# Where the second input's normalizations run, and which PSUM bank takes the first group's adapter products

## The chip, the cores and the metric

The kernel runs on one core of a Trainium2 chip. The metric is the device time of one execution in microseconds (us), as a median over executions. The engines are named as in the profile: PE (TensorE, matrix products), DVE (VectorE), ACT (ScalarE), POOL (GpSimd) and SP (SyncE, which only issues DMAs here). PSUM is the memory that PE writes its products to; the kernel uses it in banks of 128 x 512 float32.

## The reference

Two inputs x[b] of 1024 rows and 1024 columns, all in float32, go through four layers: causal attention with 32 heads of 32 and a small adapter, a feed-forward layer with a router, a second attention, and the feed-forward layer again. The change lies in the first one:

```python
x = x + attn_a(layernorm(x), w_attn, w_proj, adapter_wte, gating)

qkv = x @ w_attn.T                      # q, k, v: 32 heads of 32
q, k = rope(q), rope(k)
y = softmax(causal(q @ k.T / sqrt(32))) @ v
aq, ak, av = adapter_wte @ w_attn.T     # 10 adapter rows; ak and av are used
y = y + gating * softmax(q @ ak.T / sqrt(1024)) @ av
return y @ w_proj.T
```

The layer norm takes the mean and the variance of each row and has no weights.

## The kernel before, in words

**Attention A** works on 2 inputs (b) x 8 groups of four heads (g) x 2 halves of 512 queries (n), one `Unit` each, in that order. `attend` walks over the units in rounds. A round issues score products (tiles `sc` and `st`, two buffers in all), then the products with v, then `late`, and then it spends a fixed budget on other PE work. This other work stands in a queue of generators, the `Filler`: `project(b, g)` makes q, k and v of a group, as many groups ahead as a gate allows. Each `yield` of a number is a piece of PE work with that cost; a yielded tuple costs nothing and only marks that something is done.

**Order.** PE's and POOL's instructions keep the order in which the program writes them in this stage. The instructions of DVE, ACT and SP are put in order by the compiler's scheduler, which works by its own estimate of when operands are ready, so they can run long before their place in the program. An instruction given to `tc.keep_in_program_order` is issued behind the instruction that stands before it on its engine.

**Layer norm.** `layernorm` (L241) takes a tile of 128 rows: two `bn_stats` (L244), an aggregate (L248), a small step (L251), two steps on ACT (L253, L255), three small steps (L257 to L259) and the normalized tile (L261). With `behind=True` the first `bn_stats` alone is held in program order.

**The second input.** `normalize_ahead` (L719) loads each of its eight tiles, normalizes it and stores it to DRAM (`xnd`, L723). From group 3 to group 6 the main loop (L1002 to L1009) adds two tiles ahead of the group's projection. The tiles have the tag `t4k`, with three buffers for loads and results together. Later `second` (L727) loads the normalized tiles back and transposes them on PE, two steps a tile, into `xnT[1, n]`. `project_blocks(0, 7)` takes eight of these steps and `project_first(1)` the other eight, through `next(turnover)`.

**The banks.** Short work takes a bank from `bank` (one buffer, tag `ps`): transposes of the second input, the adapter's scores (`asc`) and their transpose, the adapter's parts, and the rows of shifts. Products of the projections take one of a pair, `ca` and `cb`: `next_bank` swaps the pair and gives the one that was used less recently, `block_bank` gives one without a swap. The adapter's keys (`akp`) and values (`avp`) are short products: before, those of group 0 take `next_bank`, those of later groups `block_bank`.

**The start.** All eight tiles of the first input are normalized; four are transposed (`half(0, 0)`, alternating banks of the pair); then `project_first(0)` makes k, the adapter's keys, q, and in `values_first` the adapter's parts and v with the adapter's values; then come the other four tiles and their products. `rotate` (L806) reads k or q from its bank on DVE (L811, L812) and ends on POOL (L815, L816).

**Adapter scores.** `late` calls `adapter_scores` in the round after a unit has begun and `adapter_rows` three rounds later. `adapter_scores` fills the `ps` bank on PE, and two steps on DVE (`am` L754, `ae` L756) read it.

Of the kernel before, what the change touches and what calls it, by code (L numbers as in the profile page):

```python
# [20 lines left out]
P = 128  # L21
# [7 lines left out]
NH = 4 * NA  # L29
# [118 lines left out]
def tile_model(ctx: ExitStack, tc: tile.TileContext, d, out: bass.AP):  # L148
# [14 lines left out]
    def block_bank(shape, name, i=0):  # L163
        return ps.tile(shape, F32, tag=pair[i], name=name)

    def next_bank(shape, name):
        pair.rotate(1)
        return block_bank(shape, name, 1)
# [72 lines left out]
    def layernorm(pl, tag, x, name, behind=False):  # L241
        stats = pl.tile([P, 2, 6], F32, tag="stats", name=f"stats_{name}", bufs=2)
        for i in range(2):
            r = dve.bn_stats(stats[:, i, :], x[:, i * HF : (i + 1) * HF])  # L244
            if i == 0 and behind:
                tc.keep_in_program_order(r)
        mv = pl.tile([P, 2], F32, tag="mv", name=f"mv_{name}", bufs=2)
        dve.bn_aggr(mv, stats)  # L248

        ve = pl.tile([P, 1], F32, tag="ve", name=f"ve_{name}", bufs=2)  # L250
        dve.tensor_scalar(ve, mv[:, 1:2], EPS, None, ALU.add)  # L251
        lv = pl.tile([P, 1], F32, tag="lv", name=f"lv_{name}", bufs=2)
        act.activation(lv, ve, AF.Ln)  # L253
        r0 = pl.tile([P, 1], F32, tag="r0", name=f"r0_{name}", bufs=2)
        act.activation(r0, lv, AF.Exp, scale=-0.5)  # L255
        e = pl.tile([P, 1], F32, tag="e0", name=f"e_{name}", bufs=2)
        dve.tensor_scalar(e, r0, r0, ve, ALU.mult, ALU.mult)  # L257
        dve.tensor_scalar(e, e, -0.5, 1.5, ALU.mult, ALU.add)
        dve.tensor_scalar(r0, r0, e, None, ALU.mult)  # L259
        xn = pl.tile([P, C], F32, tag=tag, name=f"xn_{name}")  # L260
        dve.tensor_scalar(xn, x, mv[:, 0:1], r0, ALU.subtract, ALU.mult)  # L261
        return xn
# [286 lines left out]
    def stage_a(wk, big):  # L549
# [144 lines left out]
        def x_load(b, t, pl, tag):  # L694
            xt = pl.tile([P, C], F32, tag=tag, name=f"xa{b}_{t}")
            sp.dma_start(xt, d["x"][b, t * P : (t + 1) * P, :])
            return xt
# [21 lines left out]
        def normalize_ahead():  # L719

            for t in range(NT):
                xn = layernorm(big, "t4k", x_load(1, t, big, "t4k"), f"a1_{t}")
                sp.dma_start(xnd[t], xn)  # L723
                yield ("norm", t)

        def second():
# [8 lines left out]
            for t in range(NT):  # L735
# [5 lines left out]
                    xns[t + 2] = load(t + 2)  # L741
                yield from transposed(xns.pop(t), xnT[1, n][:, :, i * P : (i + 1) * P], f"a1_{t}")

        def adapter_scores(u):
            b, g, n = u.at
            nm = f"{b}_{g}_{n}"
            qT = st["q", b, g]
            asc = bank([P, 4, NH], f"as{nm}")
            for t in range(4):
                q0 = n * HF + t * P  # L750
                mm(asc[:, t, :], lhsT=qT[:, q0 : q0 + P], rhs=aks[:, g, :], start=True, stop=True)
            s3 = asc.rearrange("p t (h j) -> p (t h) j", j=NA)
            nmx = wk.tile([P, 16], F32, tag="a16", name=f"am{nm}", bufs=2)
            dve.tensor_reduce(nmx, s3, AX.X, ALU.max, negate=True)  # L754
            e3 = wk.tile([P, 16, NA], F32, tag="ta", name=f"ae{nm}", bufs=2)
            dve.tensor_add(e3, s3, nmx[:, :, None].to_broadcast([P, 16, NA]))  # L756
            act.activation(e3, e3, AF.Exp, scale=1.0 / math.sqrt(C))
            den = wk.tile([P, 16], F32, tag="a16", name=f"ad{nm}", bufs=2)
            dve.tensor_reduce(den, e3, AX.X, ALU.add)
            dve.reciprocal(den, den)  # L760
            aw = wk.tile([P, 4, NH], F32, tag="aw", name=f"aw{nm}", bufs=2)
            pool.tensor_mul(aw.rearrange("p t (h j) -> p (t h) j", j=NA), e3, den[:, :, None].to_broadcast([P, 16, NA]))
            u.aw = aw
            return 4 * P * COL
# [8 lines left out]

        def late(r, begun):
            spent = 0.0
            for u, at in begun.items():
                if r - at == 1:
                    spent += adapter_scores(u)
                elif r - at == 4:
                    spent += adapter_rows(u)  # L780
            return spent
# [9 lines left out]
            return 2 * n * COL  # L791

        def adapter_keys(g):
            akp = block_bank([P, NH], f"akp{g}") if g else next_bank([P, NH], f"akp{g}")
            mm(akp, lhsT=parts_at.pop(f"k{g}"), rhs=tosum.rearrange("p h j -> p (h j)"), start=True, stop=True)
            dve.tensor_mul(aks[:, g, :], akp, own.rearrange("p h j -> p (h j)"))
            return NH * COL

        def adapter_values(g):
            avp = block_bank([NH, 2 * P], f"avp{g}") if g else next_bank([NH, 2 * P], f"avp{g}")  # L800
            pe.matmul(avp, lhsT=tosum.rearrange("p h j -> p (h j)"), rhs=parts_at.pop(f"v{g}"), start=True, stop=True)
            for i in range(2):
                dve.scalar_tensor_tensor(avs[:, g + i, :], avp[:, i * P : (i + 1) * P], gate[:NH], ownT, ALU.mult, ALU.mult)
            return 2 * P * COL
# [39 lines left out]
        def project_first(b, between):  # L844
            wqk = wqk_at[b, 0]
            if b == 0:
                yield adapter_parts("k0", lambda c: wqk[:, c, 1, :], P)
            else:
                assert next(turnover) is None
                yield from begin_values(b, 0)  # L850
            for n in range(2):
                if n == 1:
                    if b == 0:
                        yield from between
                    yield from begin(b, 1)
                    combine(b)
                xh = xnT[b, n]
                for s, key in ((1, "k"), (0, "q")):
                    qp = next_bank([P, HF], f"{key}p{b}_{n}")
                    for c in range(NC):  # L860
                        mm(qp, lhsT=wqk[:, c, s, :], rhs=xh[:, c, :], start=(c == 0), stop=(c == NC - 1))
                        yield HF * COL
                        if b and n == 0 and c % 2:
                            yield next(turnover)
                    rotate(b, 0, key, n, qp)
                    if b == 0 and n == 0 and key == "k":
                        yield adapter_keys(0)
                yield ("qk", b, 0, n)
                if b == 0:
                    yield from values_first(n)  # L870
            combine_first(b)

        def project_blocks(b, g):
            nm = f"{b}_{g}"
            k, q = st["k", b, g], st["q", b, g]
            if (b, g) == (0, NG - 1):
                assert next(turnover) is None
            halves = {i: (t, n) for i, t, n in ((11, k, 0), (12, k, 1), (21, q, 0), (22, q, 1))}
            places = {i: t[:, n * HF : (n + 1) * HF] for i, (t, n) in halves.items()}

            def mul(dst, left, right, start, stop):
                mm(dst, lhsT=left, rhs=right, start=start, stop=stop)
                yield HF * COL

            def settled(i):
                rotate(b, g, "k" if i < 20 else "q", halves[i][1], places[i])

            i = 0
            for r in seven(b, nm, st.pop(("f", b, g)), mul, [P, HF], places, lambda x: rotate(b, g, "k", 0, x), settled):
                if r is None:  # L890
                    if g % 2 == 0:
                        yield from begin_values(b, g)
                elif r is True:
                    yield ("qk", b, g, 0)
                else:
                    yield r
                    i += 1
                    if i == 14 and b == 0:
                        yield adapter_keys(g)
                    if (b, g) == (0, NG - 1) and i > 12 and i % 2 == 0:  # L900
                        yield next(turnover)
            yield ("qk", b, g, 1)

        def begin_values(b, g):
# [96 lines left out]
        turnover = second()  # L1001
        for b in range(B):  # L1002
            for g in range(NG):

                old = b * NG + g - 3
                if b == 0 and g >= 3:
                    fill.add(ahead_of(ahead, 2))
                fill.add(project(b, g, half(0, 1, xns) if b == g == 0 else None),
                         ("unit", f"A{old // NG}_{old % NG}_1") if old >= 0 else None)  # L1009
# [715 lines left out]
```

## Time and profile before

| | us |
|---|---|
| median of 3 runs (lowest, highest) | 2446.78 (2443.63, 2448.23) |
| the profiled execution | 2446.86 |
| its span, first instruction to last | 2445.2 |
| PE busy with products | 2374.2 |
| DVE busy | 1434.9 |
| ACT busy | 1100.3 |
| POOL busy | 591.3 |

The span runs from the first to the last instruction of the program; the 1.7 us beside it lie around the program. Attention A fills about the first half of it. "L394" is line 394 of the kernel. In the profile's lines a name such as `xn_a<-xa` is the tile written and the tile read, with the numbers of the buffers left out, and `x16` counts instructions. "idle before" is the time that an engine stood before an instruction, with the instruction that it waited for. The granted clock is the share of its full clock that PE was given.

### The profile page before, as it was taken

The page shows a single profiled execution, that of the slowest core. Times are in us where ns is not written, and L with a number is a line of the kernel's source. Part 1 is how long each engine was busy: PE and PEld are TensorE (multiplying, and loading weights), DVE is VectorE, ACT ScalarE, POOL GpSimd, SP SyncE. Part 2 cuts the span into 40 slices and gives each one's busy share as a digit, 9 for nine tenths or more (in the row PEclk, how much of TensorE's full clock was granted, in tenths as well). Part 3 has the DMA queues.
Part 4 walks back from the last instruction along what each step waited for, and adds up shares of the span by engine and source line. Part 5 has one row for each costly group of instructions (what it writes and reads, how often), then busy time and mean ns, then how long its engine had stood idle before and what let it go on. Part 6 is the DMA issues. An engine that isn't in the chain of part 4 may idle for free.

```text
span 2445.2 us, 60552 instructions
## 1 busy us (share of the span) xinstructions
PE 2374.2 (97%) x25135; PEld 1084.3 (44%) x25135; DVE 1434.9 (59%) x4310; ACT 1100.3 (45%) x2104; POOL 591.3 (24%) x927
## 2 busy tenths in 40 slices
PE   7899999999999999999999999999999999989999
PEld 4434444455354544445433444574333543223454
DVE  7666665666656666565741236567666766553453
ACT  2246666666565666566642000012445446654200
POOL 1332322222323223222211131202111112121332
PEclk9999999999999999999999999999999999999999
DMA  6632322333233333333212654532323202223543
GB/s 218 205 98 79 101 88 87 102 93 103 96 120 111 95 98 92 96 97 110 88 62 78 205 188 140 169 121 84 109 87 104 88 27 96 65 95 100 172 155 121
DMA packets 173044, 271.56 MB, mean 111 GB/s; under 512 B 16224, under 2 KB 76768, under 8 KB 172768
## 3 DMA queue, kind: packets, MB, share of 16 engines
q1 hardware_dynamic: 172768, 267.68, 34.1%
q8 instruction: 197, 3.23, 0.5%
q14 instruction: 79, 0.65, 0.1%
HBM read 212.05 MB, written 55.57 MB: 109 GB/s over the span
## 4 chain that ended last, share of the span: by engine, by line
PE 84%; DVE 9%; DMA 2%; ACT 2%; issue 1%; POOL 1%; SPq 1%; DVEq 0%; POOLq 0%
PE st L394 9%; PE sc L322 8%; PE y_A L416 5%; PE y L200 5%; PE y_f L198 4%; PE z L200 3%; PE st L392 3%; PE z_f L198 3%; PE x L200 3%; PE y_v L200 3%; PE x_f L198 2%; PE y_B L416 2%; PE y_f L200 2%; PE y_p L198 2%; DVE pr_A L335 2%; PE x_v L200 2%
## 5 line engine op out<-in xcount | busy, mean ns | idle before, releaser
L506 ACT ACTIVATE pt<-st 128x1024 f32<-128x1024 f32 (+1 forms) x418 | 425.9, 1019 | 615.3 <-PE st L394 487.2
L343 ACT ACTIVATE pr_A<-pr_A,nmax_A 128x896 f32<-128x896 f32 (+7 forms) x512 | 389.8, 765 | 56.8 <-DVE nmax_A L335 56.5
L335 DVE CUSTOM_DVE_ANT_0 pr_A<-sc,mask 128x512 f32<-128x512 f32 (+3 forms) x512 | 251.1, 537 | 196.5 <-PE st L394 99.5
L322 PE MATMUL sc<-kT,qT 32*128 32x512 f32 (+3 forms) x1536 | 327.2, 522 | 4.5 <-DVE nmax_A L335 2.3
L394 PE MATMUL st<-qT,kT 32*128 32x512 f32 (+3 forms) x1536 | 306.2, 485 | 0.0
L335 DVE CUSTOM_DVE_ANT_0 pr_A<-sc,mask,part_A 128x512 f32<-128x512 f32 (+1 forms) x256 | 156.3, 648 | 146.8 <-PE sc L322 96.5
L401 POOL TENSOR_SCALAR_AFFINE_SELECT pt<-pt 128x256 f32<-128x256 f32 x256 | 105.1, 428 | 466.4 <-ACT pt L506 466.4
L343 ACT ACTIVATE pr_B<-pr_B,nmax_B 128x1024 f32<-128x1024 f32 x128 | 145.6, 1140 | 53.1 <-DVE nmax_B L335 53.0
L239 POOL TENSOR_TENSOR xf<-xf,b_base 128x256 f32<-128x256 f32 x100 | 73.0, 760 | 378.2 <-DVE xn_f L261 328.7
L322 PE MATMUL sc<-kq,qk 32*128 32x512 f32 x512 | 146.9, 650 | 15.6 <-DVE nmax_B L335 10.0
L416 PE MATMUL y_A<-pt,v 128*32 128x512 f32 (+3 forms) x1536 | 157.0, 496 | 0.0
L394 PE MATMUL st<-rows_B,kq 32*128 32x512 f32 x512 | 144.3, 640 | 2.0 <-ACT pt L506 1.4
L394 PEld LDWEIGHTS st<-qT,kT 32*128 32x128 f32 x1536 | 133.5, 185 | 16.4 <-issue 11.3
L392 PE MATMUL st<-rows_A,ones 3*128 3x512 bf16 (+3 forms) x768 | 127.6, 329 | 4.2 <-DVE nmax_A L335 3.7
L335 DVE CUSTOM_DVE_ANT_0 pr_B<-sc,zeros,part_B 128x512 f32<-128x512 f32 x128 | 91.1, 748 | 60.0 <-PE sc L322 60.0
L335 DVE CUSTOM_DVE_ANT_0 pr_B<-sc,zeros 128x512 f32<-128x512 f32 x128 | 83.3, 687 | 69.6 <-PE sc L322 69.6
L392 PEld LDWEIGHTS <-ones 3*128 3x128 bf16 x768 | 36.7, 91 | 193.5 <-issue 186.1
L322 PEld LDWEIGHTS sc<-kT,qT 32*128 32x128 f32 x1536 | 113.3, 184 | 19.5 <-issue 5.9
L815 POOL TENSOR_TENSOR qr<-qr,sin 128x256 f32<-128x256 f32 x64 | 60.5, 945 | 227.2 <-DVE qr L811 226.2
L343 ACT ACTIVATION_READ_ACCUMULATOR pr_A<-pr_A,nmax_A 128x1 f32 x512 | 97.2, 190 | 0.0
L200 PE MATMUL y<-tt,wqk 128*32 128x512 f32 x768 | 92.6, 594 | 0.0
L416 PEld LDWEIGHTS y_A<-pt,v 128*32 128x32 f32 x1536 | 33.6, 108 | 117.8 <-issue 108.0
(429 smaller groups left out, 4229.6 us busy)
## 6 DMA issues: line engine op xcount, KB each, us to landing
tt<-td SPq DMA_DIRECT2D x252, 256.0 KB, 2.8
qkb_f<-tf SPq DMA_DIRECT2D x84, 256.0 KB, 2.9
qkb_s<-tf SPq DMA_DIRECT2D x84, 256.0 KB, 3.0
wqk<-in_w_attnT SPq DMA_DIRECT2D x32, 512.0 KB, 5.1
xf<-x SPq DMA_DIRECT2D x25, 512.0 KB, 4.3
xa<-in_x SPq DMA_DIRECT2D x16, 512.0 KB, 5.7
wv<-in_w_attnT SPq DMA_DIRECT2D x8, 1024.0 KB, 5.5
yd<-ys SPq DMA_DIRECT2D x32, 256.0 KB, 2.7
```

Source lines behind the costliest of these rows:

```text
L198: return pe.matmul(out, lhsT=lhsT, rhs=rhs, start=start, stop=stop, skip_group_check=True)
L200: pe.matmul(out[i : i + 32], lhsT=lhsT[:, i : i + 32], rhs=rhs, start=start, stop=stop, skip_group_check=True)
L239: pool.tensor_add(dst[:, i : i + 2 * P], a[:, i : i + 2 * P], b[:, i : i + 2 * P])
L322: yield w * COL, lambda: pe.matmul(dst[:, o : o + w], lhsT=self.qt[rows, qc : qc + P], rhs=self.kt[rows, c0 : c0 + w], start=True, stop=True)
L335: minimum[0] = dve.tensor_tensor_reduce(pr[:, c0 : c0 + w], sc[:, i, o : o + w], m, -self.scale, BIG if c0 == 0 else self.part[:, col], AL ...
L343: tc.keep_in_program_order(act.activation(pr[:, :nk], pr[:, :nk], AF.Exp, bias=self.nmax[:, col], scale=-1.0, accum_out=self.sums[:, col]))
L392: yield w * COL / 4, lambda: pe.matmul(dst[:, o : o + w], lhsT=of["ones"][three, :], rhs=self.rows[three, off : off + w], start=True, stop ...
L394: yield w * COL, lambda: pe.matmul(dst[:, o : o + w], lhsT=self.kt[rows, kb * P : (kb + 1) * P], rhs=rhs, start=self.extra, stop=True)
L401: pool.affine_select(out=dg, in_=dg, compare_op=ALU.is_ge, fill=0.0, base=0, pattern=[[0, 2], [1, P]], channel_multiplier=-1)
L416: pe.matmul(self.y[32 * h : 32 * h + 32, off : off + w], lhsT=self.value(h, kb), rhs=pt[h // 2][:, h % 2, o : o + w], start=self.opens, st ...
L506: act.activation(pt[:, :, low_:wide_], st[:, :, low_:wide_], AF.Exp, scale=ts[0][0].scale)
L815: pool.tensor_mul(qr[:, hs], qr[:, hs], sin[:, cols][:, hs])
```

## The change

It has three parts.

1. `normalize_ahead` calls `layernorm` with `behind=True`, and the main loop adds its tiles from group 2 to group 5.
2. Group 0's adapter keys and values take the `ps` bank.
3. The steps of `second` go through `turn_over`. Each call owes one step. If `adapter_scores` was issued in the same round, the first call after it gives none; otherwise all owed steps are given. What is still owed at the end of `project_blocks` and of the first half of `project_first` is given there.

```diff
         def normalize_ahead():
             for t in range(NT):
-                xn = layernorm(big, "t4k", x_load(1, t, big, "t4k"), f"a1_{t}")
+                xn = layernorm(big, "t4k", x_load(1, t, big, "t4k"), f"a1_{t}", behind=True)
                 sp.dma_start(xnd[t], xn)
                 yield ("norm", t)
...
+        given = [False]
+        owed = [0]
+
+        def turn_over():
+            owed[0] += 1
+            if given[0]:
+                given[0] = False
+                return
+            while owed[0]:
+                owed[0] -= 1
+                yield next(turnover)
+
         def adapter_scores(u):
+            given[0] = True
...
         def late(r, begun):
             spent = 0.0
+            given[0] = False
...
         def adapter_keys(g):
-            akp = block_bank([P, NH], f"akp{g}") if g else next_bank([P, NH], f"akp{g}")
+            akp = (block_bank if g else bank)([P, NH], f"akp{g}")
...
         def adapter_values(g):
-            avp = block_bank([NH, 2 * P], f"avp{g}") if g else next_bank([NH, 2 * P], f"avp{g}")
+            avp = (block_bank if g else bank)([NH, 2 * P], f"avp{g}")
...
                         if b and n == 0 and c % 2:
-                            yield next(turnover)
+                            yield from turn_over()
...
+                if b and n == 0:
+                    while owed[0]:
+                        owed[0] -= 1
+                        yield next(turnover)
                 yield ("qk", b, 0, n)
...
                     if (b, g) == (0, NG - 1) and i > 12 and i % 2 == 0:
-                        yield next(turnover)
+                        yield from turn_over()
+            while owed[0]:
+                owed[0] -= 1
+                yield next(turnover)
             yield ("qk", b, g, 1)
...
                 old = b * NG + g - 3
-                if b == 0 and g >= 3:
+                if b == 0 and g >= 2:
                     fill.add(ahead_of(ahead, 2))
```

## The prediction

> **What bounds the kernel now.** I read the page first. TensorE (PE) is busy nearly all the time and carries most of the chain that ended last:
>
> ```profile
> PE 2374.2 (97%) x25135; PEld 1084.3 (44%) x25135; DVE 1434.9 (59%) x4310; ACT 1100.3 (45%) x2104; POOL 591.3 (24%) x927
> PE 84%; DVE 9%; DMA 2%; ACT 2%; issue 1%; POOL 1%; SPq 1%; DVEq 0%; POOLq 0%
> ```
>
> PE's order is written out by hand, so a gap taken out of PE brings everything behind it forward, unless the next wait eats it. The page gives 2445.2 - 2374.2 = 71 us without a matmul. Where are they? The busy times by stretch (length, then PE, PEld, DVE, ACT and POOL; clock, DMA share and GB/s last):
>
> ```profile
> 0.00:160.00 160.00, 136.83 (x1125) 65.53 (x1129) 112.68 (x325) 51.19 (x139) 46.69 (x87) 0.95 0.55 186
> 160.00:560.00 400.00, 394.68 (x5958) 184.71 (x5950) 255.35 (x807) 247.93 (x500) 108.00 (x178) 1.00 0.31 91
> 560.00:680.00 120.00, 113.41 (x1384) 53.06 (x1380) 77.64 (x227) 73.05 (x144) 40.02 (x62) 1.00 0.35 111
> ```
>
> The first 160 us lose 23 us and run at a reduced clock; the 400 us after them lose 5.3. The stores of the second input's normalized tiles (xnd, L723) lie at 36.3 to 111.0 us: all eight normalizations, though written into the fill of groups 3 to 6, run in that first stretch. PE's waits from 20 to 120 us (total, times, longest):
>
> ```profile
> PE qp L198 <- DVE e_a L258: 4.1, 1, 4.1
> PE sc L322 <- DVE nmax_A L335: 2.3, 2, 2.1
> PE xt_a L204 <- DVE avs L803: 2.1, 1, 2.1
> PE xt_a L204 <- DVE xnT L232: 1.0, 1, 1.0
> PE xt_a L204 <- ACT v L952: 0.9, 1, 0.9
> PE sc L322 <- POOL qT L816: 0.6, 1, 0.6
> ```
>
> Five of the six touch what the change edits. The granted clock at three of these places, and at a fourth gap later (clock is third from the right):
>
> ```profile
> 28.00:32.00 4.00, 1.65 (x3) 0.76 (x4) 3.96 (x14) 0.81 (x4) 1.67 (x3) 0.92 0.53 199
> 32.00:36.00 4.00, 4.00 (x7) 1.65 (x6) 3.39 (x11) 0.41 (x2) 1.02 (x2) 0.65 0.00 0
> 104.00:108.00 4.00, 3.26 (x13) 2.18 (x14) 3.90 (x12) 2.24 (x6) 4.00 (x7) 0.81 0.00 0
> 108.00:112.00 4.00, 3.83 (x24) 1.61 (x27) 3.93 (x12) 2.83 (x6) 0.89 (x2) 0.76 0.06 24
> 612.00:616.00 4.00, 1.12 (x36) 0.21 (x23) 2.78 (x8) 0.30 (x2) 0.00 (x0) 1.00 0.11 35
> ```
>
> After each of the first gaps the clock dips. The loss is (0.08 + 0.35) x 4 = 1.72 us, then (0.19 + 0.24) x 4 = 1.72 us; 64 to 72 us (0.69 and 0.88) gives 1.72 again.
>
> **The change part by part.**
>
> A. *Adapter keys of group 0 leave the rotating pair.* The timeline of PE:
>
> ```profile
> 25.91 0.31 PE L198 MATMUL akp<-tosum,parts_k 128*128 128x40 f32 x2
> 30.35 8.83 PE L198 MATMUL qp<-xnT,wqk 128*128 128x512 f32 x16 [4.14 <-DVE e_a L258]
> ```
>
> The wait is put down to e_a, but it is the bank: k took one of the pair, akp the other, so q needs k's bank back, and k's last reader, kT L812, ran 29.66 to 30.30 behind six normalization steps on VectorE (DVE). With akp in the short-work bank, q takes the other of the pair, whose transpose was copied out by 19.9 us. Saved: 4.14 us, and the slow clock behind it (q took 8.83 us, k 7.13 for the same 16 instructions: 1.70). 5.8 us. What is late next? The scores at 44.20 need qT, finished on POOL at 42.34 + 1.23 = 43.57; both follow q's end, so the 0.6 us of room stays. The value weights are needed at 33.3 instead of 39.1; DMA is idle at 32 to 36 us (share 0.00), so they had landed.
>
> B. *Adapter values leave the pair, and DVE is free in the second half's transposes.* Idle there: 0.94 (first transpose in the bank of the last value product) + 2.09 (avs L803, DVE late) + 1.00 (copy xnT at 64.87, behind a second-input xn of 0.81) + 0.14 = 4.17, plus the clock dip of 1.72. The order of banks shifts by one, so the second transpose now waits for the copy of the last value product; that copy ended about 1.45 us after the product and 1.2 us of PE work lie between, and two banks drained by copies of 0.59 and 0.69 still leave small gaps: I leave 1.0 us. 4.17 + 1.72 - 1.0 = 4.9 us.
>
> C. *No second-input normalization in front of the scores at 102.6 us.* The timeline of DVE:
>
> ```profile
> 101.96 0.69 DVE L244 BATCH_NORM_STATS2 stats_a<-xa 128x6 f32<-128x512 f32 x1 [4.53 <-DMA xa<-in_x]
> ```
>
> DVE stood 4.53 us for a tile of x, with the score rows (L335) queued behind; PE then waited 2.12 + 0.17. With the dip of 1.72: 4.0 us.
>
> On the clock, the rows say that a stretch of slow clock follows gaps of 4.14, about 4 in pieces, and 2.12 us, but not the 3.38 us before 616. The Trainium skill, "TensorE: Matmul & The Clock Gate", section "Part 1: The HAM clock gate", says that the clock halves only after a whole idle window of about 3.4 us. By that rule only A's dip goes, and the sum below is 3.4 us smaller; the trace disagrees at 102.6 us, so I keep the rows.
>
> D. *Transposes put off after adapter scores.* Only one of the 16 turnover steps falls in the round of an adapter_scores: the transpose at 616.50 waits 3.38 us for the readers (am, ae) of the same bank. They end at 616.40 because DVE waited 2.37 us for wv from 610.85. Put off by two of k's products (1.88 us together), the transpose still finds the bank taken for 1.5 us, and the two that are then owed share one bank, so the second waits for a copy, 0.59 + 0.2. 3.38 - 1.5 - 0.8 = 1.1 us saved; between -0.8 (only the second wait comes) and 3.4.
>
> E. *Eight normalizations at their place.* Per tile DVE runs two bn_stats (0.65 each), 0.20, 0.15, 0.27, 0.14, 0.20 and xn 0.81: 3.1 us, 24.8 in all, moved into 150 to 400 us, in pairs after the projections of groups 1 to 4, which end near 149, 234, 306 and 385 us. Queued behind them are score rows and rotations. Low bound: the 160 to 560 stretch loses 5.3 us of PE for 255 us of DVE, so 24.8 more would lose 0.5. High bound: the same helper with its first bn_stats held, from 1700 to 2260 us (20 tiles):
>
> ```profile
> DVE stats_f L244 <- DMA xf<-x: 15.5, 5, 4.7
> PE sc L322 <- DVE nmax_B L335: 10.0, 7, 2.8
> PE sc L322 <- DVE part_B L335: 5.6, 4, 3.5
> ```
>
> 15.6 us of PE for 20 tiles is 0.78 each, 6.2 for eight. Only the first bn_stats is held; the second may still be drawn ahead and wait for its tile, and that is what the first row shows. I take the middle, 3.4 us, as DVE is 64% busy there and the loads find DMA at 0.31 instead of 0.55.
> The rest of a tile: two ACT steps of 0.20 (3.2 us in all, ACT 62% busy): nothing, PE's copies are not behind them for longer than that. Two DMAs on SP: the next x load waits for the store of the tile before (3.2 us to land) with the tt loads behind it; five tt tiles are ahead, and PE uses two per round of about 4 us, 10 us of cover: nothing. Were the cover gone, 3.2 us for each of three pairs, 9.6.
> Starting at group 2 instead of 3 alone costs no PE step.
>
> **Sum.** 5.8 + 4.9 + 4.0 + 1.1 - 3.4 = 12.4 us. The profiled execution took 2446.86 us (span 2445.2 and 1.7 around it), 0.1 above the median of 2446.78: 2434.5 us.
>
> **Rivals.**
> 1. *The clock by the rule*: two of three dips stay. 12.4 - 3.4 = 9.0: 2437.9 us. Chance 0.08; 616 us speaks for it, 102.6 against.
> 2. *They float all the same*, since x loads and second bn_stats stay free: C and half of B stay, E costs nothing. 5.8 + 2.4 + 1.1 = 9.3: 2437.6 us. 0.05: an xn can't pass its held bn_stats.
> 3. *The next wait takes it*: DVE stays late at the start with the first input's own tiles and factors (15.84 of 20 us busy at 20 to 40), so A keeps only 4.1, B nothing, C 2.3, D 1.1, and E costs the full 6.2: 1.3 us, 2445.6. 0.15.
> 4. *Slower: the free bn_stats blocks DVE.* As at 97 us, DVE stands for a late x tile and PE loses 2.12 + 1.72 = 3.8 us, now in a stretch that was clean. Gains are 15.8 without E, so it decides from the fifth tile on, and passes +0.2% at the sixth; all eight give 30.4 - 15.8 = 14.6 more: 2461.5 us. For it: the five waits of 15.5 us above. Against: two of eight tiles are loaded early, and two of eight waited before, on busier DMA. 0.10.
>
> **Numbers.** A measurement of this kernel can tell about 0.2% (4.9 us). Forecast 0.62, rivals 1 and 2 0.13: faster 0.75. Rival 3: same 0.15. Rival 4: slower 0.10. Low end: D at 3.4 and E at 0.5 give 17.6, so 2429; high end: rival 3 with 2446.
>
> **What would show it.** Right: q begins within 0.3 us of akp and takes about 7.1 us; no xnd store before 140 us; the clock at 1.00 through 28 to 36 and 104 to 112; PE busy in 0 to 160 up by about 11 us of idle. Wrong: DVE waits for xa after 150 us with PE gaps on nmax_A or part_A behind them, or a new PE wait between 36 and 60 us.

## The result: about half of the forecast gain, and the profile after

| | before | after |
|---|---|---|
| median of 17 runs each (lowest, highest), us | 2445.65 (2441.15, 2449.81) | 2439.28 (2433.36, 2443.13) |
| profiled execution, us | 2446.86 | 2443.13 |
| its span, us | 2445.2 | 2441.4 |

The ratio of after to before is 0.9972, with a 95% interval of 0.9965 to 0.998: 6.8 us of 2445 (4.9 to 8.6). The forecast was 12.4 us. The profiled execution of after happens to be the longest of its 17, so the two profiles differ by 3.7 us only; sizes below that rest on profiles alone are marked so.

The page of after, the two lines that answer to those of before (busy time by engine, and the shares of the chain that ended last):

```profile
PE 2377.8 (97%) x25147; PEld 1084.3 (44%) x25147; DVE 1429.7 (59%) x4310; ACT 1100.3 (45%) x2104; POOL 591.6 (24%) x927
PE 86%; DVE 9%; DMA 2%; ACT 2%; issue 1%; POOL 0%; SPq 0%; DVEq 0%; POOLq 0%
```

These averages hide what happened. Busy times by stretch (columns as before; the clock is third from the right):

```profile
0.00:160.00 160.00, 146.64 (x1271) 68.06 (x1271) 101.98 (x312) 56.34 (x149) 46.34 (x88) 0.99 0.46 147
160.00:560.00 400.00, 389.57 (x5844) 182.31 (x5844) 263.50 (x828) 245.55 (x494) 108.47 (x177) 0.98 0.35 107
```

The first 160 us now have PE busy for 146.64 instead of 136.83, at a clock of 0.99 instead of 0.95. The next 400 lose 10.4 us instead of 5.3, at 0.98 instead of 1.00. So there is a gain and a loss, one behind the other. To size both, I follow one PE instruction that both kernels issue, the first shift product (`st_A`) of a round, at two places. It waits about 0.6 us in both kernels, so it is a fair mark. From PE's timeline, before and then after:

```profile
174.69 0.41 PE L200 MATMUL st_A<-identb,shift 128*32 128x128 bf16 x16 [0.61 <-DVE ae L756]
445.50 0.41 PE L200 MATMUL st_A<-identb,shift 128*32 128x128 bf16 x16 [0.63 <-DVE ae L756]
```

```profile
158.78 0.41 PE L200 MATMUL st_A<-identb,shift 128*32 128x128 bf16 x16 [0.61 <-DVE ae L770]
442.17 0.41 PE L200 MATMUL st_A<-identb,shift 128*32 128x128 bf16 x16 [0.63 <-DVE ae L770]
```

After is ahead by 174.69 - 158.78 = 15.9 us at the first mark and by 445.50 - 442.17 = 3.3 at the second: 12.6 us are given back in between.

The gain first. PE's waits from 20 to 120 us were six rows and are now one, and q begins right behind the adapter's keys and takes 7.11 us instead of 8.83 (waits, then PE's timeline, then the clock by stretch):

```profile
PE xt_a L204 <- ACT xnT L234: 0.2, 1, 0.2
```

```profile
26.94 0.31 PE L198 MATMUL akp<-tosum,parts_k 128*128 128x40 f32 x2
27.08 7.11 PE L198 MATMUL qp<-xnT,wqk 128*128 128x512 f32 x16
```

```profile
32.00:36.00 4.00, 4.00 (x26) 1.86 (x25) 3.78 (x10) 0.00 (x0) 2.45 (x4) 1.00 0.01 4
108.00:112.00 4.00, 4.00 (x44) 1.33 (x40) 2.99 (x9) 3.97 (x7) 0.48 (x2) 1.00 0.16 57
```

Of the 15.9 us, 1.5 are neither A, B nor C: both kernels have a short wait of PE for POOL's qT (1.32 us before, 1.50 after), and the slow clock behind it lasted 6.8 us in this execution of before and 3.4 in that of after, at half speed. That is 1.7 us less lost, and 0.2 more waited. It leaves 14.4, where A, B and C came to 5.8 + 4.9 + 4.0 = 14.7. (The first 160 us gained 146.64 - 136.83 = 9.8 us of busy PE. The prediction's sign said about 11, though its own gaps, 4.1 + 3.2 + 2.3, add up to 9.6.)

Then the loss. PE's waits from 160 to 450 us, of after (first fence, the three rows that grew) and of before (second fence; it has no row for ve_a and none for sc):

```profile
PE st L392 <- DVE nmax_A L335: 4.0, 3, 2.5
PE st_A L200 <- DVE ve_a L251: 2.4, 1, 2.4
PE sc L322 <- DVE part_A L335: 1.7, 1, 1.7
```

```profile
PE st L392 <- DVE nmax_A L335: 2.7, 3, 1.2
```

The new gaps begin at 215.28 us (2.50 instead of 1.23), 300.38 (1.72) and 382.69 (2.39); with a 0.34 at 212.41 PE is idle for 5.7 us more than before in this stretch. Each of the three is followed by half clock:

```profile
216.00:220.00 4.00, 2.22 (x14) 0.71 (x17) 3.37 (x9) 2.07 (x6) 0.77 (x2) 0.75 0.69 274
304.00:308.00 4.00, 4.00 (x52) 1.13 (x48) 1.07 (x7) 1.69 (x6) 0.77 (x2) 0.50 0.13 46
384.00:388.00 4.00, 2.92 (x30) 1.07 (x34) 3.42 (x12) 0.63 (x3) 0.46 (x1) 0.66 0.43 132
```

By the clock rows around them, the slow stretches last 3.4, 6.8 and 3.4 us, half of which is lost: 6.8 us. Together 5.7 + 6.8 = 12.5, which is the 12.6 given back.

What DVE does at the second of these gaps (DVE's timeline, then PE's):

```profile
296.90 1.28 DVE L244 BATCH_NORM_STATS2 stats_a<-xa 128x6 f32<-128x512 f32 x2
...
299.12 0.27 DVE L257 TENSOR_SCALAR e_a<-r_a,ve_a 128x1 f32<-128x1 f32 x1 [0.51 <-ACT r_a L255]
...
299.86 0.81 DVE L261 TENSOR_SCALAR xn_a<-xa,mv_a,r_a 128x1024 f32<-128x1024 f32 x1
300.59 0.42 DVE L335 CUSTOM_DVE_ANT_0 pr_A<-sc,mask 128x256 f32<-128x256 f32 x1
```

```profile
302.10 0.48 PE L322 MATMUL sc<-kT,qT 32*128 32x256 f32 x2 [1.72 <-DVE part_A L335]
```

From 296.90 to 300.59 DVE runs one normalization from end to end, with the round trip to ACT (0.51 us of standing still) inside it, and the score rows (L335) come only then. PE's next scores need the buffer that those rows read. At 215.28 it is only the second half of a normalization: its four last steps run from 214.96 to 216.51, and the score rows (L335) begin at 216.42. At 382.69 the wait is put down to ve_a, but the late steps are the adapter's `am` and `ae`, which ran at 384.36 and 384.70 behind an xn of 0.81, a set of score rows and two bn_stats (DVE's timeline, then PE's):

```profile
383.16 1.28 DVE L244 BATCH_NORM_STATS2 stats_a<-xa 128x6 f32<-128x512 f32 x2
384.36 0.31 DVE L768 TENSOR_REDUCE am<-as 128x16 f32<-128x160 f32 x1
384.58 0.20 DVE L248 BATCH_NORM_AGGREGATE mv_a<-stats_a 128x2 f32<-128x12 f32 x1
384.70 0.32 DVE L770 TENSOR_TENSOR ae<-as,am 128x160 f32<-128x160 f32 x1
```

```profile
385.08 0.47 PE L200 MATMUL st_A<-identb,shift 128*32 128x128 bf16 x16 [2.39 <-DVE ve_a L251]
```

DVE hardly stood for the loads of x there. Its row among DVE's waits from 100 to 450 us:

```profile
DVE stats_a L244 <- DMA xa<-in_x: 0.7, 2, 0.4
```

### The profile page after: what moved, and what is told of

The parts are those of the page before. It is cut to its first block, busy times and chain, and to the rows that moved or that the text cites. A ratio compares the mean times of both kernels' runs of the same rounds, so it can differ in the third digit from the quotient of the medians.

```text
span 2441.4 us, 60572 instructions
## 1 busy us (share of the span) xinstructions
PE 2377.8 (97%) x25147; PEld 1084.3 (44%) x25147; DVE 1429.7 (59%) x4310; ACT 1100.3 (45%) x2104; POOL 591.6 (24%) x927
## 4 chain that ended last, share of the span: by engine, by line
PE 86%; DVE 9%; DMA 2%; ACT 2%; issue 1%; POOL 0%; SPq 0%; DVEq 0%; POOLq 0%
PE st L394 9%; PE sc L322 8%; PE y_A L416 5%; PE y L200 5%; PE y_f L198 4%; PE z L200 4%; PE st L392 3%; PE z_f L198 3%; PE x L200 3%; PE y_v L200 3%; PE x_f L198 3%; PE y_B L416 2%; PE y_f L200 2%; PE y_p L198 2%; DVE pr_A L335 2%; PE x_v L200 2%
## 5 line engine op out<-in xcount | busy, mean ns | idle before, releaser
L335 DVE CUSTOM_DVE_ANT_0 pr_A<-sc,mask 128x512 f32<-128x512 f32 (+3 forms) x512 | 251.4, 537 | 193.7 <-PE st L394 92.2
L335 DVE CUSTOM_DVE_ANT_0 pr_A<-sc,mask,part_A 128x512 f32<-128x512 f32 (+1 forms) x256 | 156.2, 647 | 147.5 <-PE sc L322 96.7
L394 PEld LDWEIGHTS st<-qT,kT 32*128 32x128 f32 x1536 | 133.8, 185 | 16.6 <-issue 11.6
L335 DVE CUSTOM_DVE_ANT_0 pr_B<-sc,zeros 128x512 f32<-128x512 f32 x128 | 83.3, 687 | 72.4 <-PE sc L322 72.3
L335 DVE CUSTOM_DVE_ANT_0 pr_B<-sc,zeros,part_B 128x512 f32<-128x512 f32 x128 | 91.0, 747 | 58.4 <-PE sc L322 58.4
```

The costliest lines, as they stand in the source:

```text
L335: minimum[0] = dve.tensor_tensor_reduce(pr[:, c0 : c0 + w], sc[:, i, o : o + w], m, -self.scale, BIG if c0 == 0 else self.part[:, col], AL ...
L394: yield w * COL, lambda: pe.matmul(dst[:, o : o + w], lhsT=self.kt[rows, kb * P : (kb + 1) * P], rhs=rhs, start=self.extra, stop=True)
```

## The experiments

Two theories stood at the start. **Mine**: the starting gains are as worked out, and E is larger because a whole normalization, with its round trip to ACT, stands on DVE ahead of the score rows. **The rival**: it is the free second bn_stats that is drawn ahead and blocks DVE (rival 4 at a smaller price). Ratios are to the kernel before, measured beside each experiment.

**Each part alone.** e1_banks is before with part 2:

```diff
-            akp = block_bank([P, NH], f"akp{g}") if g else next_bank([P, NH], f"akp{g}")
+            akp = (block_bank if g else bank)([P, NH], f"akp{g}")
...
-            avp = block_bank([NH, 2 * P], f"avp{g}") if g else next_bank([NH, 2 * P], f"avp{g}")
+            avp = (block_bank if g else bank)([NH, 2 * P], f"avp{g}")
```

> Part 2 alone: group 0's adapter keys and values in the short-work bank, everything else as before. Theory (the start gains by banks and by normalizations separately): q follows the adapter keys within 0.3 us and takes about 7.1 us (5.8 us); of the transposes' 4.2 us of idle the 0.94 and 2.09 go and the 1.00 behind a second-input xn stays; the 2.12 us at the scores near 100 us stays. Together 7 to 9 us faster than before (ratio 0.9963 to 0.9971), that is as fast as the whole change or a little faster, since the cost of the moved normalizations is not paid. Rival (the next wait takes it): DVE still has the second input's tiles at the start, so PE meets it later in new waits before 130 us: 1 to 3 us faster (0.9988 to 0.9996).

Measured: 2436.85 against 2444.65, ratio 0.9973 (0.9962 to 0.9983), 6.6 us. At the first mark its profile is 7.45 us ahead, 5.7 without the difference behind the qT wait. A's wait is gone, B's and C's are not:

```profile
PE xt_a L204 <- ACT xnT L234: 2.4, 1, 2.4
PE sc L322 <- DVE nmax_A L335: 2.2, 1, 2.2
```

At the second mark it is still 7.4 ahead. It gives nothing back.

e2_norms is before with part 1:

```diff
-                xn = layernorm(big, "t4k", x_load(1, t, big, "t4k"), f"a1_{t}")
+                xn = layernorm(big, "t4k", x_load(1, t, big, "t4k"), f"a1_{t}", behind=True)
...
-                if b == 0 and g >= 3:
+                if b == 0 and g >= 2:
```

> Part 1 alone: the second input's normalizations held from group 2 on, everything else as before. Theory (each moved normalization holds the score rows behind it on DVE and the clock dips after the gap): the 4.1 us wait of q stays, the start gains 6 to 7 us (the 1.00, part of the 2.09, the 2.12 and their dips), and the stretch from 160 to 450 us loses 9 to 12 us as in the whole change: 2 to 6 us slower than before (1.001 to 1.0025). Rival (the start's gain belongs to the normalizations, the banks only moved with them): 3 to 6 us faster (0.9975 to 0.9988).

Measured: 2445.24 against 2444.65, ratio 1.0004 (0.9995 to 1.0013): no difference that shows. Its profile is 10.2 us ahead at the first mark (8.7 without the qT difference), and it then has the same gaps as after: 2.51, 1.72 and 2.39 us, 11.3 given back up to the second mark. What it won it lost again; it was expected to be slower, but the start won 8.7 us instead of the 6 to 7 expected. And 5.7 + 8.7 = 14.4, just what the whole change has at the first mark: the banks bring A, the normalizations bring B and C.

e3_turnover is before with part 3 (the `turn_over` lines of the change, nothing else).

> Part 3 alone: the second input's transposes put off after adapter scores, everything else as before. Theory (of the 3.4 us gap near 613 us, 1.5 us of the wait for DVE stay, and the second of the two owed transposes waits 0.7 us for the bank's copy): two gaps of 1.5 and 0.7 us in place of one of 3.4, 1.1 us faster than before, which the times can hardly tell from no change (0.9985 to 1.0005). Rival (DVE reads the scores earlier once PE doesn't stand): only the 0.7 us are left, 2.7 us faster. Rival (two pieces in one bank cost more than the wait): 0 to 1 us slower, a second gap over 1.5 us.

Measured: 2442.78 against 2444.78, ratio 0.9995 (0.9986 to 1.0005), below what these runs tell apart. In the profile the two transposes near 613 us wait 1.44 and 0.68 us in place of the one wait of 3.38, but the clock falls to 0.90 and 0.68 from 612 to 620 us, which costs 1.7 us.

**What in the normalization costs.** e4_copy is the whole change, with each second-input normalization cut to one held step of about xn's size. It leaves out the statistics, the two ACT steps and the scaling, so it does not compute the layer; loads and stores stay:

```diff
-                xn = layernorm(big, "t4k", x_load(1, t, big, "t4k"), f"a1_{t}", behind=True)
+                x = x_load(1, t, big, "t4k")
+                xn = big.tile([P, C], F32, tag="t4k", name=f"xn_a1_{t}")
+                tc.keep_in_program_order(dve.tensor_copy(xn, x))
```

> The whole change, but each second-input normalization is replaced by one held DVE copy of the tile (the statistics, the two ACT steps and the scaling are left out); loads, stores and their places stay. Theory (burst on DVE): one step of 0.8 us instead of eight steps with a round trip to ACT, so the gaps near 215, 300 and 383 us go or shrink below 1 us: 7 to 11 us faster than the whole change, 2428 to 2432 us where before takes 2445.7 (0.993 to 0.9945). Rival (loads and stores in SP's queue, or DVE standing for a tile of x): the DMAs are all still there, so no change against the whole change: 2439 us (0.997).

Measured: 2427.98 against 2444.65, ratio 0.9931 (0.9917 to 0.9944), 16.9 us. Between the marks 2.7 us are given back instead of 12.6, the longest PE gap there is 1.39 us, and there is no slow clock. The same loads and stores at nearly the same places cost little; the steps between them are the price.

e5_spread keeps the whole computation, but hands it out in pieces. A new `layernorm_steps` is `layernorm` with a `yield` between the pieces; the first step of each piece, and the second bn_stats, are held:

```diff
-                xn = layernorm(big, "t4k", x_load(1, t, big, "t4k"), f"a1_{t}", behind=True)
-                sp.dma_start(xnd[t], xn)
+                x = x_load(1, t, big, "t4k")
+                steps = layernorm_steps(big, "t4k", x, f"a1_{t}")   # bn_stats | bn_stats, aggregate, ACT | e, e, r | xn
+                for step in (1, 1, 0, 1):
+                    fill.chore(("N", t), (lambda steps=steps: next(steps)) if step else (lambda: None))
+                fill.chore(("N", t), lambda steps=steps, t=t: sp.dma_start(xnd[t], next(steps)))
```

The `Filler` runs one chore behind each piece of PE work, so score rows can stand between the pieces, and ACT has one free place in the chain for its two steps.

> The whole change, with each second-input normalization cut into four held pieces (first bn_stats; second bn_stats with the aggregate and the ACT steps; the three small steps; xn and its store) that are given one after each piece of other PE work, with one piece of PE work between the ACT steps and what needs them. The work is the same. Theory (it is the chain in one piece that costs, not its sum): score rows get in between, the three gaps shrink to under 0.7 us each and the dips behind them go: 5 to 10 us faster than the whole change, 2430 to 2434 us (0.9935 to 0.995). Rival (the 25 us of DVE work cost wherever they lie): no change, 2437 to 2441 us. Rival (loads and stores): the same as that.

Measured: 2427.98 against 2444.65, ratio 0.9936 (0.9923 to 0.9949), 15.6 us. Its interval lies wholly under that of the change (0.9965 to 0.998), so it beats both kernels, and it came out below the 2430 to 2434 us expected; the ratios differ by 0.0036, 8.8 us (roughly 5 to 12 by the two intervals). DVE's timeline where the chain stood in one piece before:

```profile
292.89 0.15 DVE L273 TENSOR_SCALAR ve_a<-mv_a 128x1 f32<-128x1 f32 x1
...
294.44 0.42 DVE L359 CUSTOM_DVE_ANT_0 pr_A<-sc,mask 128x256 f32<-128x256 f32 x1 [1.40 <-PE st L418]
...
295.82 0.27 DVE L280 TENSOR_SCALAR e_a<-r_a,ve_a 128x1 f32<-128x1 f32 x1
...
296.57 0.81 DVE L285 TENSOR_SCALAR xn_a<-xa,mv_a,r_a 128x1024 f32<-128x1024 f32 x1
297.71 0.42 DVE L359 CUSTOM_DVE_ANT_0 pr_A<-sc,mask 128x256 f32<-128x256 f32 x1 [0.33 <-PE sc L346]
```

Score rows (L359 here) run between ve_a and e_a, as soon as PE has made them, and DVE waits for PE rather than PE for DVE. Between the marks 0.7 us are given back (16.6 ahead, then 15.9), and no slow clock lies there. The first mark itself waits 1.10 us here instead of 0.61, so the price of the pieces is nearer 1.2 us.

**The rival.** e7_both_held is the whole change with the second bn_stats of these tiles held too:

```diff
-            if i == 0 and behind:
+            if behind and (i == 0 or name.startswith("a1_")):
```

> The whole change, with the second bn_stats of each second-input tile held in program order too. Theory (the chain in one piece costs, DVE stands for a tile of x only 0.7 us in all from 100 to 420 us): the gaps near 215, 300 and 383 us stay within 1 us of what they were, time as the whole change within 2 us (0.9965 to 0.998). Rival (the free bn_stats at the head of DVE's queue costs): those gaps go, 6 to 12 us faster than the whole change (0.992 to 0.9947).

Measured: 2441.38 against 2444.78, ratio 0.9986 (0.9976 to 0.9995), not better than the change. The three gaps are there at 2.71, 1.72 and 2.86 us, and there is a new one of 1.42 us at the first pair. With e5, which also holds both but cuts the chain, the rival falls: it is not where the second bn_stats stands but what stands with it. Two things change together in e5: the chain is cut, and its pieces come later, behind other PE work. The runs don't tell these apart.

**Where, and whether to hold at all.** e6_group3 is the whole change with `g >= 3` kept.

> The whole change, but the held normalizations start at group 3 as before instead of group 2. Theory (each pair costs what DVE carries where it lies; the pair near 136 us cost nothing in the whole change): that pair goes, and one comes near 440 us, so gaps near 215, 300 and 383 us stay in kind and a fourth of 1 to 2.5 us may come: 0 to 4 us slower than the whole change (2439 to 2443 us where before takes 2445; 0.997 to 0.9988). Rival (the early pair disturbs the rotations at 136 us): 2 to 4 us faster than the whole change.

Measured: 2438.86 against 2444.78, ratio 0.9976 (0.9966 to 0.9986), no difference from the change that shows. The pairs that now run near 215, 300 and 383 us have gaps of 2.51, 1.72 and 2.39; the last pair, up to 463 us, has none of its own. So in this form the place sets the gap, not which tiles run there.

e8_not_held is the whole change without `behind=True`.

> The whole change without the hold: the second input's normalizations are added from group 2 on, but none of their instructions is held in program order. Theory (the hold moves them, not the place in the program): they run in the first 110 us again, and the kernel is the one with the banks alone, with the turnover's 1 us: 2436 to 2438 us where before takes 2445 (0.996 to 0.9975), no gap near 300 and 383 us. Rival (the place alone is enough): xnd stores lie after 130 us and the time is that of the whole change with its three gaps, 2438 to 2441 us.

Measured: 2434.86 against 2444.78, ratio 0.9961 (0.9949 to 0.9974), 9.5 us; its interval overlaps that of the change. The stores of the normalized tiles, of after and then of e8 (lowest, median and highest issue time in ns; first and last start in us):

```profile
L723 SPq DMA_DIRECT2D xnd<-xn_a x8: 319/320/339, 141.7 to 387.9; - x8
```

```profile
L723 SPq DMA_DIRECT2D xnd<-xn_a x8: 326/328/3620, 37.9 to 109.8; - x8
```

Without the hold the tiles run in the first 110 us as before, and the gaps near 300 and 383 us are gone. So it is the hold that moves them, and the move as made buys nothing that these runs can tell.

## Why the prediction was right or wrong, step by step

- **A, right.** The bank was the cause, as argued against the row's own name for it (e_a). (DVE's timeline of before has eight normalization steps, not six, between 27.21 us and k's last reader at 29.66; the argument is the same.) e1 alone is 5.7 us ahead at the first mark, without the qT difference; 5.8 were forecast. By the ratios it has as much as the whole change (6.6 and 6.8 us).
- **B and C, right together** at 8.7 us in e2 (8.9 forecast). The 1.0 us left over for B was too much: PE is idle for 0.5 us in after from 54 to 62 us, where these transposes run. But I put a part of B down to the banks; e1 shows 0.60 + 2.44 of it still there, so it was the normalizations.
- **D, right as a wait, lost as a time.** The two waits in after, from PE's timeline, are the 1.5 and about 0.8 of the prediction, in place of 3.38; behind them after's profile has a slow stretch (clock 0.75 and 0.83 from 612 to 620 us) that costs 1.7, as e3's has, and before has none there. What the clock does there differs by kernel, and e3's interval (-3.4 to +1.2 us) holds the forecast and zero.

```profile
613.04 0.63 PE L204 MATMUL xt_a<-ident,xn 128*128 128x128 f32 x4 [1.53 <-issue]
614.34 1.11 PE L204 MATMUL xt_a<-ident,xn 128*128 128x128 f32 x4 [0.68 <-ACT xnT L234]
```

- **E, the step that failed: mis-sized.** Forecast 3.4 us, at most 6.2. It is 8.8 by the ratios of e5 and the change, and 12.6 in the profiled execution. The idle time of PE there, 5.7 us, lies within the bounds, though near the upper one and not in the middle. What the sum left out is the slow clock behind the new gaps, 6.8 us in the profile, although A, B and C had counted it behind theirs. The row it was taken from (20 tiles, 15.6 us of waits) gave waits and no clock. The clock also goes with the spread of the runs: the mean clock is 0.993 in the fastest of after (2433.36 us) and 0.989 in the slowest (2443.13), and 0.004 of 2440 us is 9.8 us, as much as they differ by (the clock is given to three digits, so 7 to 12 us).
- **Rival 1, the clock by the rule,** is refuted at its own places: the slow stretches at 64 to 72 and 104 to 112 us went with their gaps. The Trainium skill, "TensorE: Matmul & The Clock Gate", section "Part 1: The HAM clock gate", has the clock halve after a whole idle window of about 3.4 us; here it halved after gaps of 1.72 and 2.39 us.
- **Rival 2, they float all the same,** did not happen with the hold; without it (e8) the gain was 9.5 us, and the rival's sum was 9.3. That they agree is in part luck: at the first mark e8's profile is 7.8 us ahead, 6.1 without the qT difference, so of B little came with A.
- **Rival 3, the next wait takes it,** failed at the start, where nothing took A, B or C, but its last term (E at its full bound) came true and more.
- **Rival 4, the free bn_stats blocks DVE,** has the place nearly right and the mechanism wrong: DVE stood 0.7 us for x in all, and holding the second one (e7) did not help.

What stays open: why the same chain costs a gap at three of the places and none near 142 and 463 us, beyond that PE's next need differs there; how much of the price is the round trip to ACT, how much the length of the chain and how much its place; and the 0.8 us by which the profiles' lead grows from 677 us (2.9) to the end (3.7).

## What to carry to other kernels

When work is moved onto an engine that others wait for, don't price it by its busy time: ask how long the longest piece is that nothing else can enter, round trips to other engines included, and cut it into pieces that the urgent steps can pass between. Here the same steps at the same loads cost some 9 us as they stood and about 1 us in pieces given later. And if a slow clock was counted behind the gaps that a change removes, it must be counted behind those it makes.

## What the runs showed of the hardware

The length of a gap does not tell whether the clock drops behind it. Wait of the transpose near 616 us in before, with the clock at 1.00 through 612 to 624 us, and the same wait in e2, with the clock at 0.82 in the 4 us around its end and 0.75 in the next 4:

```profile
616.50 0.63 PE L204 MATMUL xt_a<-ident,xn 128*128 128x128 f32 x4 [3.38 <-issue]
```

```profile
617.52 0.63 PE L204 MATMUL xt_a<-ident,xn 128*128 128x128 f32 x4 [3.34 <-issue]
```

Yet the 1.72 us wait near 300 us was followed by 6.8 us of half clock in after, e2, e6 and e7, and the 1.3 to 1.5 us wait for qT near 136 to 151 us by 3.4 or 6.8 us in all kernels but e3. Nor does the same gap behave alike in two kernels: the one of 2.50 us near 216 us is followed by a slow clock in after and in e6, but not in e7 (2.71 us) nor in e2, whose PE line and clock rows are:

```profile
223.49 0.39 PE L392 MATMUL st<-rows_A,ones 3*128 3x512 bf16 x2 [2.51 <-DVE nmax_A L335]
```

```profile
220.00:224.00 4.00, 1.49 (x20) 0.88 (x18) 3.33 (x10) 2.57 (x6) 1.23 (x3) 1.00 0.77 300
224.00:228.00 4.00, 4.00 (x48) 1.16 (x40) 3.38 (x12) 2.55 (x8) 0.41 (x1) 1.00 0.51 192
```

By these rows a sum can take the clock's price of such a gap only as a range, here from nothing to 3.4 us. The slow stretches come in lengths of 3.4 and 6.8 us (worked out from the clock rows at half speed), as if whole windows were judged whose edges fall where they will. The same section of the Trainium skill calls the window free-running, 3.4 us long: the lengths agree with it. What makes a window count as idle when PE rests for only part of it, these runs do not show.
